# A two-layer graph network on one core: the output bias moves from VectorE to GpSimd, three opening loads change queue, and all steps get a new order

## The chip, the cores and the metric

The kernel runs on one core of a Trainium2 chip. The core has five engines with a queue of instructions each: TensorE (PE in the profile; its weight loads are listed as PEld), VectorE (DVE), ScalarE (ACT), GpSimd (POOL) and SyncE (SP), which here only issues DMAs. An engine works through its queue in order; engines wait for each other by semaphores. SBUF is the on-chip memory of 128 partitions, PSUM the banks that TensorE writes to. The metric is the device time of one execution in microseconds (us).

## The reference

The input is x, 128 graphs of 128 nodes with 256 features, and one 0/1 matrix adj of 128 x 128 for each graph. Everything is float32. Layer 0 is an attention block with 8 heads whose values depend on the adjacency, a residual and norm, and a Gelu feed-forward with 1024 hidden features. Layer 1 is two graph attention steps without a nonlinearity between them, a residual and norm, and a Relu feed-forward:

```python
def layer0(src, adj):
    q, k = heads(src @ Wq + bq), heads(src @ Wk + bk)
    attn = softmax(q @ k.T / sqrt(32))
    out = sum((attn * (adj == r)) @ heads(src @ Wv[r] + bv[r]) for r in range(4))
    x = ln(src + out @ Wo + bo, g1, beta1)
    return ln(x + gelu(x @ W1 + b1) @ W2 + b2, g2, beta2)

def gat(h, adj, W, a):
    Wh = h @ W
    e = leaky_relu(Wh @ a[:256] + (Wh @ a[256:]).T, 0.2)
    return softmax(where(adj > 0, e, NEG), axis=1) @ Wh

def layer1(x, adj):
    h = gat(gat(x, adj, W1, a1), adj, W2, a2)
    h = ln(x + h, g_ln1, b_ln1)
    return ln(h + relu(h @ w_ff1 + b_ff1) @ w_ff2 + b_ff2, g_ln2, b_ln2)
```

## The kernel before

The 16384 tokens are worked through in 32 groups of 4 graphs (512 tokens). A group passes through a fixed set of stages, each written as a Python generator that emits a few instructions per step:

- `in` loads the transposed x (xT, 512 KB), `rest` loads adj (256 KB) and then x (512 KB). All three are issued from SP's queue.
- `bo` is `prepared` (L687 on): two adds of the output bias to the incoming x, one for each pair of graphs, 128 x 512 elements each, in place, and a square of adj on ScalarE for a later check. The bias row `bo` has been enlarged by the value bias once at the start (`output_bias`). Its sum with x is the residual of the attention.
- `q` makes queries, keys and values. From group 2 on it is `projected`, with the seven-product scheme of Strassen and Winograd for a 2 x 2 split of each product (forms B11, B21, B22, T1 to T4 of a weight, L789).
- `a` is `attention`: scores into PSUM (ps, L859), exponentials on ScalarE (e, L866), the mask products `pm` = e times adj on VectorE (L876), the products with the values (pav, L975), reciprocals of the sums, the output product (pwo, L1021) and the add of the residual x (L416). `d` is `folded`, which sums the exponentials with copies by DMA.
- `n0` to `n3` are the norms: statistics (L407, L409), a root whose add is on VectorE (L430) and whose power is on GpSimd (L431), and two affine passes on VectorE (L445). `n0` to `n2` then copy x as two planes of 16 bits on ScalarE (L465) and transpose them by DMA from SP's queue (L468); `t0` to `t2` put the words together on ScalarE (yT, L493).
- `f` and `fc` are the two halves of the first feed-forward, `k` and `kc` of the second (products L525 and L534), again with the seven-product scheme. `seeded` is a PSUM bank that ScalarE fills with an earlier product before further products are added to it; `p` and `h` are copies and differences between the products.
- `l` is the graph attention layer (pw L1098, py L1111, pg L1124), `out` the store, `z` the last norm.

The order of the work is written out by hand as three strings of tokens, FRONT, STEADY and TAIL. A token such as `bo:1` asks for the next step of stage `bo` of the group that is one ahead of the current base; `*3` repeats. STEADY is run for bases 1 to 29. The strings fix the order of the instructions within each engine's queue; between engines only the data dependencies and the reuse of buffers hold. So several groups are in work at a time: in STEADY the second feed-forward of group g-1, the graph layer of group g, the first feed-forward of group g+1 and the projections and scores of group g+2 lie side by side.

At the start `Weights` issues the loads. Loads that are put in a list (`to("qk")` and so on) are issued one by one by tokens such as `Lqk` from SP's queue; bq, bk, the row of value biases, its first row as columns (b0) and bo are issued at once from ScalarE's queue before any token.

x has three buffers (pool `io`), adj three, xT one. GpSimd's queue holds, in a steady group, four powers and nothing else.

Of the kernel before, what the change touches and what calls it, by code (L numbers as in the profile page):

```python
# [120 lines left out]


FRONT = """
Lqk in:0 Lqk q:0 Lqk Lv q:0 L1 q:0 Lv q:0 Lqk L1 in:1 Lv q:0 Lv_ q:0*2 Lv q:0 rest:0 Lv_ a:0*3 L1
q:0 d:0 a:0 Lv_ a:0 d:0 a:0*2 d:0 L1*2 d:0 q:0 d:0*2 Lh1 d:0 a:0 d:0 a:0 q:0*2 rest:1 q:0*2
rest:0 wqk a:0*7 q:1 L2 w1 a:0 L4 a:0*3 q:1*2 d:0 bo:0 d:0 Lgat Lg1 a:0*2 d:0*2 q:1 L2 Lg1 d:0 w1
d:0 q:1 bo:0 q:1 q:0 d:0 Lo q:1 d:0 q:0 q:1 bo:0 a:0*4 L1 a:1 a:0*2 a:1 a:0 rest:1 wqk w1 a:0
a:1*2 a:0 a:1 L3 a:1 Lg1 d:1 a:0 d:1 Lg1 d:1 a:1 a:0*2 q:1 a:0*2 Lg2 d:1 Lgat n0:0 b1 d:1*2 L2
a:1 d:1 n0:0 q:1 b1 q:1 n0:0 L4 q:1 wqk d:1 q:1 Lgat n0:0 a:1 b1 output_bias n0:0 wv L2 q:1
n0:0*2 t0:0 b1 a:1 output_bias t0:0 a:1 Lh1*2 a:1*3 Lgat a:1*2 gw f:0 a:1 t0:0 a:1 b1 L3 a:1 b1  # L130
w2 a:1 t0:0 w1 t0:0*2 d:1 fc:0 b1 gw q:1 Lg2 d:1*3 a:1 f:0 fc:0 f:0 b1 f:0 a:1 fc:0*3 d:1 L4 d:1
f:0 q:1 fc:0 f:0 fc:0 f:0 d:1 f:0 Lh2 gw L3 a:1 f:0 d:1 a:1 f:0*2 a:1 fc:0 a:1 fc:0*2 bo:1 w2
bo:1 fc:0*2 a:1*3 f:0 a:1 wqk fc:0 in:2 fc:0 gw a:1 L3 f:0 a:1 fc:0 f:0 fc:0*2 a:1 f:0 w2 a:1 Lh1
bo:1 a:1 L3 a:1 f:0 fc:0*3 f:0 wv n0:1 L3 fc:0 q:2 f:0 fc:0 c1 fc:0 f:0 n0:1 q:2 fc:0 w2 n0:1
fc:0 q:2 n0:1 t0:1 n0:1 f:0 c1 t0:1 fc:0 f:0 L4 fc:0 c1 n0:1 fc:0 wv fc:0 f:0*2 n0:1 q:2 fc:0 q:2
f:0 fc:0*2 q:2 n1:0*2 gw n1:0 Lh2 n1:0 q:2 t0:1 n1:0*2 c1 n1:0 q:2 t0:1 c1 u1 f:1 q:2*3 t0:1 c1
f:1 t1:0*2 c1 l:0 gelu u2 fc:1 t1:0 l:0 t0:1 t1:0 l:0*2 fc:1 f:1 l:0 fc:1 l:0*2 fc:1 l:0 q:2 l:0
f:1*3 fc:1*3 f:1*3 fc:1 rest:2 fc:1*2 q:2*2 exp q:2 fc:1 l:0*2 u1 l:0 q:2 u1 q:2 f:1 q:2 l:0 fc:1
f:1 l:0 a:2 l:0 u2 l:0 fc:1 l:0*3 a:2 f:1 fc:1*2 a:2 l:0 fc:1 l:0 a:2*2 l:0*3 a:2 l:0*2 u2 u1 d:2
l:0 d:2 l:0 fc:1 f:1 l:0 f:1 wv f:1*2 fc:1*2 l:0 d:2 fc:1 l:0 d:2 f:1 a:2 l:0 u2 q:2 l:0 fc:1 c1  # L140
l:0*2 fc:1 q:2 l:0*2 f:1 l:0*2 d:2*2 l:0 q:2 fc:1 q:2*2 l:0 f:1 d:2 q:2 l:0*2 q:2 l:0*2 q:2 l:0
n2:0 q:2*2 d:2 n2:0 fc:1*2 q:2 f:1 n2:0*2 d:2 fc:1 n2:0*2 a:2 fc:1 f:1 n2:0 fc:1 q:2 t2:0 f:1
rest:2 t2:0 q:2 fc:1 t2:0*2 fc:1 k:0 a:2 q:2 a:2*3 d:2 fc:1 f:1 kc:0 a:2 d:2 t2:0 a:2 k:0 f:1 a:2
k:0 a:2 k:0 a:2 t2:0 fc:1 a:2 d:2*2 kc:0 a:2 kc:0 a:2 d:2 a:2 k:0 a:2 k:0 d:2 n1:1 a:2 d:2 a:2
k:0 n1:1 k:0 kc:0
# [4 lines left out]
k:-1*2 l:0*2 kc:-1 a:1*2 kc:-1 l:0 kc:-1 l:0 a:1 kc:-1 l:0 kc:-1*2 l:0*2 kc:-1 k:-1 a:1 n0:1  # L150
kc:-1 k:-1 n0:1*2 kc:-1 k:-1 n0:1 bo:1 n0:1 q:2 k:-1 kc:-1 n0:1*2 kc:-1 l:0 kc:-1 l:0 k:-1
kc:-1*2 q:2 l:0 q:2 l:0*2 t0:1*2 q:2 kc:-1 l:0 rest:2 f:1 k:-1 l:0 t0:1*2 q:2*2 l:0*2 fc:1 q:2
gelu l:0 t0:1 l:0 f:1*3 t0:1 l:0*2 fc:1 l:0 f:1 l:0*3 k:-1 q:2 f:1 fc:1 l:0 kc:-1 l:0 f:1 fc:1
f:1*2 q:2 n3:-1 l:0 fc:1*3 q:2 fc:1 f:1 fc:1*3 q:2 fc:1*2 f:1 q:2 f:1 q:2 n3:-1 fc:1*2 f:1*2 q:2
l:0 fc:1 l:0*2 f:1 q:2 l:0 fc:1*2 f:1 n3:-1 fc:1 l:0 q:2 fc:1 q:2*2 f:1 fc:1 out:-1 l:0 a:2 fc:1
l:0*2 f:1 l:0*2 a:2*2 l:0 a:2*2 l:0 d:2 q:2 a:2 q:2 d:2*2 f:1 a:2 fc:1 l:0*4 d:2 l:0 n2:0 q:2
d:2*2 q:2 fc:1*2 q:2 n2:0 q:2 f:1 n2:0*3 q:2 d:2 fc:1 q:2 n2:0 q:2 d:2 f:1 n2:0 fc:1*2 q:2 d:2
f:1 fc:1 q:2 t2:0*2 a:2 t2:0*2 q:2 a:2 q:2 f:1 q:2 fc:1 t2:0*2 k:0 f:1 exp a:2 fc:1 kc:0 d:2
a:2*2 rest:2 a:2 k:0 kc:0 d:2 a:2 k:0*2 kc:0 a:2 k:0 d:2*2 a:2 d:2 a:2 d:2 a:2 fc:1 a:2*4 d:2 a:2
# [3 lines left out]
n1:0 k:-1 kc:-1 n1:0*2 kc:-1 d:1*2 a:1 k:-1 kc:-1 a:1 d:1 k:-1 bo:1 a:1 kc:-1*4 d:1 kc:-1 n1:0
k:-1 n1:0 a:1 t1:0*2 k:-1 kc:-1 k:-1 l:0 bo:1 a:1 kc:-1 l:0*2 kc:-1 k:-1 l:0 kc:-1 a:1 t1:0 a:1
t1:0 l:0 a:1 k:-1 a:1 l:0 kc:-1*2 l:0*2 kc:-1 a:1 kc:-1 l:0 kc:-1 bo:1 k:-1 kc:-1*2 a:1*2 k:-1
kc:-1 n0:1*2 k:-1 n0:1*2 k:-1 n0:1 l:0 n0:1 l:0 n0:1 l:0 kc:-1 l:0 t0:1 k:-1 l:0 kc:-1 l:0 kc:-1
t0:1 kc:-1*2 l:0 k:-1 l:0 kc:-1 l:0 gelu l:0 f:1 t0:1 l:0 t0:1 k:-1 l:0 kc:-1 l:0 t0:1*2 l:0 f:1
fc:1*2 kc:-1 l:0 fc:1 f:1*2 k:-1 fc:1 f:1 n3:-1 l:0*2 fc:1 f:1*2 l:0 fc:1 n3:-1 l:0 fc:1 l:0 f:1
fc:1 f:1 l:0 fc:1 f:1 fc:1 l:0*2 fc:1 l:0 fc:1 l:0*3 fc:1*2 f:1*2 fc:1 f:1 l:0*4 fc:1 f:1 l:0
fc:1 f:1*2 fc:1 l:0*2 fc:1 l:0 fc:1 f:1 l:0*2 f:1 fc:1*2 n2:0 f:1 n2:0 fc:1*2 n2:0*2 fc:1 f:1  # L170
n2:0 f:1 n2:0*2 t2:0*2 fc:1*2 f:1 fc:1 t2:0 fc:1*2 f:1*2 fc:1*2 n1:1 t2:0 k:0 t2:0 k:0 kc:0 n1:1
t2:0 k:0 n1:1 k:0 n1:1 kc:0 n1:1 k:0 kc:0 n1:1*2 t1:1*2 kc:0 k:0*3 t1:1 k:0 l:1*2 t1:1 l:1 kc:0
n3:-1 l:1 kc:0*2 l:1*3 kc:0*2 l:1 kc:0 l:1 kc:0 k:0 kc:0 l:1*4 kc:0 l:1*3 k:0 l:1 kc:0 l:1 k:0*3
kc:0 l:1*5 kc:0 l:1 kc:0 k:0 l:1*5 k:0 l:1 kc:0 l:1 k:0 l:1*2 kc:0*3 l:1*2 kc:0 k:0 l:1*6 kc:0
k:0 l:1*3 kc:0 l:1*2 k:0 n2:1 kc:0 n2:1*5 kc:0*2 k:0 kc:0 n2:1 k:0 kc:0 k:0 t2:1*2 kc:0*2 k:1
t2:1*3 kc:1 t2:1 k:1 kc:1 k:1 checks k:1 kc:1 k:1 kc:1 k:1 kc:1 k:1 kc:1*2 k:1 kc:1*3 k:1 k:0
kc:1*2 kc:0 k:1*2 kc:1 k:1 kc:1*2 k:1 kc:1 k:1*2 kc:1 k:1*2 kc:1 n3:0 kc:1*2 k:1 kc:1 exp kc:1*2
n3:0*2 kc:1*2 out:-1 k:1*3 kc:1*3 k:1 kc:1 k:1 kc:1 out:0 k:1 z:1*2 kc:1*2 z:1*2
# [11 lines left out]
def fast_pass(ctx, tc, a, out):  # L190
# [494 lines left out]
    gelu, exp = lambda: table(AF.Gelu), lambda: table(AF.Exp)  # L685

    def prepared(S):  # L687
        g, xr, ad = S["g"], S["x"], S["ad"]
# [10 lines left out]
        yield 1
# [888 lines left out]
```

## Time and profile before

| | |
|---|---|
| time, median of 3 runs | 2611.95 us (2609.13 to 2613.82) |
| time of the profiled execution | 2611.15 us |
| its span | 2609.4 us |
| granted TensorE clock, mean | 0.997 |
| busy PE / PEld / DVE / ACT / POOL | 2566.4 / 2286.5 / 2329.3 / 1883.0 / 142.1 us |
| DMA, mean share and rate | 71 GB/s over 16 engines, 31% of their span |

The span is the time from the first to the last instruction of the profiled execution. Busy time is a union over an engine's instructions; matmuls are pipelined and their ends are modelled, so a matmul's listed duration is longer than the distance to the next one. A line of the timeline has the start, the duration, the engine, the line of the kernel, the operation, what it writes and reads, and the shape; in brackets stands the idle time of the engine before it and what ended it. A line of the groups has the number of instructions, then busy time and the mean ns of one, then the idle time before them.

### The profile page before, as it was taken

To read this page: it belongs to the slowest core of one execution; us is meant where nothing else is said; L and a number is where in the kernel's file an instruction comes from. 1 tells how busy PE (TensorE), PEld (TensorE's weight loads), DVE (VectorE), ACT (ScalarE), POOL (GpSimd) and SP (SyncE) were. 2 spreads that over 40 slices of the span, in tenths; PEclk is the share of its full clock that TensorE was granted. 3 is DMA by queue.
4 is the path that set the end of the run, shared out by engine and by line. 5 is a ranking of instruction groups with operands and counts; after the bars stand their busy time and mean duration, and the time that the engine had idled before them with its cause. 6 is when DMAs were issued, how large, how long until landed. Compare 5 with 4: busy or idle time off the path is not lost.

```text
span 2609.4 us, 54584 instructions
## 1 busy us (share of the span) xinstructions
PE 2566.4 (98%) x20362; PEld 2286.5 (88%) x20362; DVE 2329.3 (89%) x6041; ACT 1883.0 (72%) x3841; POOL 142.1 (5%) x137
## 2 busy tenths in 40 slices
...
DMA packets 317375, 186.36 MB, mean 71 GB/s; under 512 B 230448, under 2 KB 272560, under 8 KB 317104
## 3 DMA queue, kind: packets, MB, share of 16 engines
...
q8 instruction: 162, 2.65, 0.4%
...
## 4 chain that ended last, share of the span: by engine, by line
PE 83%; ACT 7%; DVE 5%; DMA 3%; issue 1%; SPq 1%; POOL 0%; DVEq 0%; ACTq 0%; POOLq 0%
PE ph L525 14%; PE po L534 14%; PE seeded L534 12%; PE seeded L525 11%; PE pqqa L789 4%; PE pvqa L789 4%; PE pav L975 4%; PE pw L1098 4%; PE pqqb L789 3%; PE pvqb L789 3%; PE pwo L1021 3%; ACT e L866 3%; PE ps L859 3%; PE pg L1124 2%; PE py L1111 2%; ACT hT L549 1%
## 5 line engine op out<-in xcount | busy, mean ns | idle before, releaser
L493 ACT COPY yT<-pT 128x512 uint16<-128x512 uint16 x384 | 271.3, 764 | 107.8 <-DMA pT<-planes 106.4
L465 ACT COPY planes<-x 128x512 uint16<-128x512 uint16 x384 | 218.3, 615 | 137.2 <-DVE x L445 135.5
L431 POOL TENSOR_TENSOR rs<-rs,mhalf 128x4 f32<-128x4 f32 x129 | 140.0, 1085 | 2406.7 <-DVE rs L430 1893.4
L525 PE MATMUL seeded<-yS,w_L_gnn_w_ff 128*128 128x256 f32 x768 | 203.5, 387 | 1.4 <-ACT p L629 0.7
L525 PE MATMUL seeded<-yS,w_L_gnn_W 128*128 128x256 f32 x768 | 199.9, 383 | 1.5 <-DVE hT L633 1.1
L525 PE MATMUL ph<-yT,w_L_gnn_W 128*128 128x256 f32 x768 | 198.1, 381 | 0.6 <-ACT yT L493 0.6
L407 DVE BATCH_NORM_STATS2 st<-x 128x6 f32<-128x256 f32 x512 | 190.1, 413 | 2.5
L534 PEld LDWEIGHTS po<-w_L_gnn_W,hT 128*128 128x128 f32 x1536 | 186.1, 192 | 6.7 <-ACT hT L549 2.1
L525 PE MATMUL ph<-yT,w_L_gnn_w_ff 128*128 128x256 f32 x768 | 187.7, 379 | 3.2 <-ACT seeded L648 2.1
L534 PE MATMUL po<-w_L_gnn_W,hT 128*128 128x128 f32 x1536 | 187.1, 275 | 1.7 <-ACT hT L549 1.7
L534 PE MATMUL po<-w_L_gnn_w_ff,hT 128*128 128x128 f32 x1536 | 187.1, 275 | 0.0
L534 PEld LDWEIGHTS po<-w_L_gnn_w_ff,hT 128*128 128x128 f32 x1536 | 181.7, 192 | 1.7
L525 PEld LDWEIGHTS seeded<-yS,w_L_gnn_w_ff 128*128 128x128 f32 x768 | 139.3, 190 | 38.2 <-ACT seeded L648 9.5
L876 DVE TENSOR_TENSOR pm<-e,adj 128x512 f32<-128x512 f32 x256 | 169.2, 682 | 0.4 <-ACT e L866 0.2
L525 PEld LDWEIGHTS seeded<-yS,w_L_gnn_W 128*128 128x128 f32 x768 | 142.8, 190 | 28.0 <-ACT seeded L648 6.4
L866 ACT ACTIVATE e<-ps 128x512 f32<-128x512 f32 x256 | 139.4, 602 | 34.8 <-PE ps L859 29.1
L525 PEld LDWEIGHTS ph<-yT,w_L_gnn_w_ff 128*128 128x128 f32 x768 | 143.5, 190 | 22.1 <-ACT seeded L648 2.5
L525 PEld LDWEIGHTS ph<-yT,w_L_gnn_W 128*128 128x128 f32 x768 | 141.7, 190 | 21.6 <-ACT seeded L621 1.2
L903 ACT COPY es<-e 32x512 f32<-32x512 f32 x240 | 147.1, 613 | 4.5
L549 ACT ACTIVATE hT<-hT,c_L_gnn_b_ff 128x256 f32<-128x256 f32 x256 | 115.9, 501 | 39.4 <-DVE hT L592 36.7
L621 ACT COPY seeded<-ph 128x512 f32<-128x512 f32 x64 | 37.4, 584 | 135.9 <-DVE x L667 135.2
L1098 PE MATMUL pw<-wu,yT 128*128 128x260 f32 x512 | 133.2, 389 | 2.3 <-ACT wh L1103 1.3
...
## 6 DMA issues: line engine op xcount, KB each, us to landing
...
es<-e SPq DMA_DIRECT2D x240, 64.0 KB, 2.0
pm<-e SPq DMA_DIRECT2D x240, 64.0 KB, 2.0
ea<-e SPq DMA_DIRECT2D x240, 64.0 KB, 2.0
...
```

The costliest lines, as they stand in the source:

```text
L407: nc.vector.bn_stats(st[:, b % 2, :], S["x"][:, b, :])
L431: nc.gpsimd.tensor_tensor(rs[:, bs], rs[:, bs], k.mhalf[:, bs], op=ALU.pow)
L465: nc.scalar.copy(planes[:, :, b], words)
L493: nc.scalar.copy(o.rearrange("p (b t h) -> p h b t", b=2, h=2), pT[:, :, :, c, :])
L525: nc.tensor.matmul(bank[:, s * TH : (s + 1) * TH], wa[:, form, 0, f * P : (f + 1) * P], m, start=start and s == 0, stop=True, skip_group_c ...
L534: nc.tensor.matmul(bank[:, s * P : (s + 1) * P], m[:, f, s * P : (s + 1) * P], wb_[:, form, f, :], start=start and s + f == 0, stop=True, ...
L549: nc.scalar.activation(o[:, s], o[:, s] if src is None else src[:, s * TH : (s + 1) * TH], func, bias=ba[:, f : f + 1],)
L789: nc.tensor.matmul(bank[:, s * TH : (s + 1) * TH], *ops, start=start and s == 0, stop=True, skip_group_check=True,)
L866: nc.scalar.activation(e[:, s], pss[s], AF.Exp, scale=SCALE)
L876: nc.vector.tensor_mul(pm[:, s], S["e", p][:, s], S["ad"][:, pair(p), None, :].to_broadcast([P, 2, NCH, P]),)
L903: nc.scalar.copy(es[own, 0], flat_e[own, s])
L1098: nc.tensor.matmul(pw[:, :NU], yT[:, c, b * P : (b + 1) * P], wu[:, c, :], start=(c == 0), stop=(c == NCH - 1),)
```

## The change

Three edits are made together.

1. In `prepared` the two adds of the bias are issued on GpSimd for groups 2 to 31, and on VectorE for groups 0 and 1 as before.
2. The load of xT of group 0 is split in two DMAs of 256 KB. The loads of the value biases' row, of b0 and of bo go from ScalarE's queue into a list of their own, `b`, whose three steps are issued from SP's queue by the token `Lb`.
3. FRONT, STEADY and TAIL are replaced. STEADY begins at another point of the group's cycle, with the end of `t2` and the values' last products, and holds the same steps.

```diff
@@ prepared
         for p in range(G // 2):
-            nc.vector.tensor_add(xr[:, pair(p)], xr[:, pair(p)], over(bo, 2))
+            (nc.vector if g < 2 else nc.gpsimd).tensor_add(
+                xr[:, pair(p)], xr[:, pair(p)], over(bo, 2)
+            )
@@ entered
-        nc.sync.dma_start(
-            xt, xT[:, g * T : (g + 1) * T].rearrange("(c p) t -> p c t", p=P)
-        )
+        cols = xT[:, g * T : (g + 1) * T].rearrange("(c p) t -> p c t", p=P)
+        for c in range(NCH) if g == 0 else (slice(0, NCH),):
+            nc.sync.dma_start(xt[:, c], cols[:, c])
@@ loads
     bq, bk = k.col("L0_gnn_bq"), k.col("L0_gnn_bk")
+    k.queue = nc.sync
+    to("b")
     bvs, bv = k.row("L0_gnn_bv", 2 * D, cut(2 * D)), k.tile([P, D], "bv")
     b0 = cut(NCH)
-    k.load(nc.scalar, b0, a["L0_gnn_bv"][0].rearrange("(c p) -> p c", p=P))
+    k.load(nc.sync, b0, a["L0_gnn_bv"][0].rearrange("(c p) -> p c", p=P))
     bo = k.row("L0_gnn_bo")
-    k.queue = nc.sync
     to("qk")
@@ FRONT (its first tokens)
-Lqk in:0 Lqk q:0 Lqk Lv q:0 L1 q:0 Lv q:0 Lqk L1 in:1 Lv q:0 Lv_ q:0*2 Lv q:0 rest:0 Lv_ a:0*3 L1
+in:0 Lqk Lv Lqk q:0 Lqk Lv q:0 Lqk q:0 in:1 Lv q:0*2 Lv_ q:0 L1 Lv q:0*2 rest:0 Lb a:0*2 Lb a:0
...
@@ STEADY before: the second attention's mask products, n1's root, the bias adds
-k:0 n1:1 kc:0 a:2 k:0 n1:1 k:0
-n1:0 k:-1 n1:0 kc:-1 n1:0 d:1*2 a:1 k:-1 kc:-1 d:1 a:1 kc:-1*2 bo:1 a:1 d:1 a:1 kc:-1 a:1*4
-kc:-1*3 n1:0 in:2 kc:-1 n1:0 k:-1 t1:0*2 kc:-1 k:-1*2 t1:0 k:-1 l:0*2 k:-1 kc:-1*2 bo:1 t1:0
...
@@ STEADY after: the same steps
+t2:-1 q:1 rest:1 t2:-1 fc:0 q:1 f:0 k:-1 a:1 q:1 d:1 a:1*2 fc:0 a:1 kc:-1 t2:-1 a:1 k:-1 d:1
+a:1*3 k:-1 t2:-1 kc:-1*2 d:1 a:1 d:1 k:-1*2 a:1 d:1 fc:0 k:-1 a:1*2 n1:0 a:1*2 k:-1 d:1*2 a:1*2
+n1:0 kc:-1 k:-1 n1:0*2 k:-1 kc:-1 k:-1 n1:0 d:1*2 a:1*2 kc:-1 d:1 a:1 kc:-1 bo:1 kc:-1 d:1 a:1
+kc:-1 a:1*3 rest:2 a:1 kc:-1*3 n1:0*2 k:-1 t1:0 kc:-1 k:-1 t1:0 kc:-1 k:-1*2 t1:0 l:0*2 t1:0 k:-1
+kc:-1 k:-1*2 l:0 kc:-1 in:2 l:0 bo:1 kc:-1 a:1*2 kc:-1 l:0 kc:-1 a:1 kc:-1 l:0*2 a:1 k:-1 l:0*2
...
```

More of the change, by code (lines that the diff above doesn't have):

```diff
@@ L123 @@
 FRONT = """
-Lqk in:0 Lqk q:0 Lqk Lv q:0 L1 q:0 Lv q:0 Lqk L1 in:1 Lv q:0 Lv_ q:0*2 Lv q:0 rest:0 Lv_ a:0*3 L1
[L125 to L145, printed above, removed]
+in:0 Lqk Lv Lqk q:0 Lqk Lv q:0 Lqk q:0 in:1 Lv q:0*2 Lv_ q:0 L1 Lv q:0*2 rest:0 Lb a:0*2 Lb a:0
+Lv_ a:0 L2 d:0 wqk a:0*2 d:0*3 q:0 L1 Lv_ q:0 a:0 L1 q:0*2 Lb d:0*2 a:0 q:0 rest:1 d:0*2 a:0 q:0
@@ new lines @@
+a:0*2 L1 a:0*4 L1 Lg1 a:0*3 q:1 a:0*2 q:1 Lgat d:0 rest:0 d:0 w1 a:0*2 q:1 q:0 Lgat L1 d:0*2 Lg2
+q:0 d:0 bo:0 q:1*2 d:0*2 Lo a:0 d:0 q:1*2 a:0*2 Lg1 a:0 L2 bo:0 q:1 a:1 wqk L4 w1 a:1 a:0 a:1*2
+Lg1 a:1 a:0*2 a:1 a:0 L2 a:0 Lg1 d:1*4 Lgat w1 a:1 a:0*2 Lh1 a:0*2 b1 a:0 d:1 q:1 n0:0 d:1 rest:1
+q:1 b1 q:1 n0:0 a:1 d:1 n0:0 q:1 n0:0 L4 d:1 L4 a:1 b1 n0:0*2 q:1 n0:0 b1 a:1 L2 q:1 L3 b1 t0:0*2
+a:1*2 gw w1 Lh1 f:0 a:1*2 Lh1 output_bias d:1 a:1*3 t0:0 d:1 output_bias Lg2 t0:0 a:1 t0:0 q:1
+d:1 b1 fc:0 f:0 t0:0 q:1 bo:0 fc:0 bo:1 fc:0 f:0 a:1 w2 a:1 f:0 b1 a:1 b1 f:0 fc:0 f:0 Lgat d:1
@@ new lines @@
+a:1 fc:0*2 w2 f:0 fc:0*2 f:0*2 d:1 Lh2 f:0 a:1 gw fc:0*4 f:0 d:1 L3 fc:0 d:1*2 f:0 a:1 fc:0 f:0
+w2 f:0 wv wqk fc:0 a:1*2 Lh1 L3 fc:0 f:0 fc:0 a:1*2 fc:0*2 a:1 f:0 a:1 bo:1 wv a:1 fc:0 a:1*3 f:0
+a:1 gw fc:0 in:2 q:2 rest:2 fc:0 q:2*2 a:1 n0:1 q:2 fc:0 f:0 fc:0 n0:1 L3*2 n0:1 L3 fc:0 n0:1 f:0
+n0:1 q:2 c1 w2 bo:1 q:2 n0:1 gw f:0*2 fc:0*4 f:0 n0:1 f:0 wv t0:1 f:0 fc:0 q:2 fc:0*2 t0:1*2 n1:0
+L4 t0:1 n1:0 gw Lh2 q:2 n1:0*2 c1 n1:0 f:1 n1:0*2 q:2 c1 u2 q:2 c1 t0:1 fc:1 q:2 c1 t1:0*2 t0:1
+c1 f:1 fc:1 u2 f:1 l:0*2 f:1 t1:0 l:0 t1:0 l:0*2 gelu fc:1 l:0*3 f:1 q:2 fc:1 l:0 f:1 fc:1*2 q:2
@@ L146 @@
+wqk fc:1 f:1 u1 f:1 fc:1 q:2 fc:1 q:2*2 exp u2 q:2*2 c1 l:0 fc:1 l:0 a:2 l:0*2 fc:1 l:0 a:2 f:1
+l:0 u1 f:1 a:2 q:2 l:0 d:2 fc:1 l:0 a:2 l:0*2 fc:1 a:2 l:0 u2 l:0*4 u1 wv l:0 fc:1 l:0*3 fc:1 l:0
+f:1 d:2 fc:1 d:2 c1 q:2 d:2 fc:1 a:2 u1 f:1*3 q:2 fc:1 f:1*2 fc:1 f:1 l:0*3 fc:1*2 q:2 a:2 l:0*2
+fc:1 l:0 q:2 f:1*2 fc:1 l:0 d:2*2 l:0 q:2 l:0*2 q:2 l:0 f:1 l:0 q:2 d:2 l:0 f:1 l:0*3 d:2 fc:1
+q:2 l:0 n2:0 fc:1*2 q:2 n2:0 d:2 n2:0 fc:1 n2:0 fc:1 n2:0*3 f:1 fc:1 t2:0 a:2 q:2 f:1 t2:0
 """
 STEADY = """
-n1:0 k:-1 n1:0 kc:-1 n1:0 d:1*2 a:1 k:-1 kc:-1 d:1 a:1 kc:-1*2 bo:1 a:1 d:1 a:1 kc:-1 a:1*4
@@ L149 @@
-kc:-1*3 n1:0 in:2 kc:-1 n1:0 k:-1 t1:0*2 kc:-1 k:-1*2 t1:0 k:-1 l:0*2 k:-1 kc:-1*2 bo:1 t1:0
[L150 to L159, printed above, removed]
-k:0 n1:1 kc:0 a:2 k:0 n1:1 k:0
+t2:-1 q:1 rest:1 t2:-1 fc:0 q:1 f:0 k:-1 a:1 q:1 d:1 a:1*2 fc:0 a:1 kc:-1 t2:-1 a:1 k:-1 d:1
```

42 lines of the change are left out of this document (26 added, 16 removed).

## The prediction

> **What bounds the kernel now.** I read the page's busy shares first, then three stretches of the span, then the chain that ended last, then one group's period in order of time.
>
> ```profile
> PE 2566.4 (98%) x20362; PEld 2286.5 (88%) x20362; DVE 2329.3 (89%) x6041; ACT 1883.0 (72%) x3841; POOL 142.1 (5%) x137
> ```
>
> ```profile
> 0.00:140.00 140.00, 127.64 (x997) 100.75 (x998) 97.63 (x263) 85.51 (x169) 6.18 (x11) 0.99 0.47 120
> 140.00:2440.00 2300.00, 2290.62 (x18309) 2054.93 (x18309) 2098.90 (x5418) 1700.65 (x3471) 125.70 (x116) 1.00 0.32 71
> 2440.00:2609.40 169.40, 148.12 (x1060) 130.83 (x1058) 132.77 (x362) 96.84 (x202) 10.23 (x10) 0.97 0.19 43
> ```
>
> The columns of the second fence are the stretch, its length, then busy time of PE, PEld, DVE, ACT, POOL, the granted clock, the DMA share and GB/s. PE is the bound: in the middle it is idle for 2300 - 2290.62 = 9.4 us. It is idle for 12.4 us in the opening and 21.3 us at the end. The matmuls are the same before and after, so the change can only move PE's idle time and its small delays.
>
> The chain shows the period, from one group's four exponentials to the next:
>
> ```profile
> 1645.28 2.05 ACT e L866 x4
> 1725.33 2.05 ACT e L866 x4
> 1804.47 2.05 ACT e L866 x4
> ...
> 2122.12 2.05 ACT e L866 x4
> 2201.11 2.06 ACT e L866 x4
> ```
>
> The shortest is 2201.11 - 2122.12 = 78.99 us; 1645 to 1725 takes 80.05. From 373.10 to 2438.65, 26 periods, the mean is 79.44. So at most some 0.45 us a group, 13 us over 29 steady groups, comes back if every group runs like the best one.
>
> The next view splits the group from 2045.1 us on into two stretches:
>
> ```profile
> 2045.10:2071.30 26.20, 26.01 (x240) 23.59 (x240) 25.72 (x66) 14.38 (x28) 1.42 (x2) 1.00 0.42 85
> 2071.30:2124.10 52.80, 52.77 (x393) 47.48 (x392) 46.70 (x125) 44.58 (x94) 2.91 (x3) 1.00 0.28 65
> ```
>
> For 26 us out of 79, DVE is as full as PE (25.72 of 26.20 us). This stretch runs from the second attention's product pg to the second pav (L975), and ends so:
>
> ```profile
> 2070.58 0.17 DVE L430 TENSOR_SCALAR rs<-mv 128x4 f32<-128x4 f32 x1
> 2070.65 0.69 DVE L876 TENSOR_TENSOR pm<-e,adj 128x512 f32<-128x512 f32 x1
> 2070.89 1.31 POOL L431 TENSOR_TENSOR rs<-rs,mhalf 128x4 f32<-128x4 f32 x1 [19.66 <-DVE rs L430]
> 2071.25 0.68 DVE L592 TENSOR_TENSOR hT<-ph,p 128x512 f32<-128x512 f32 x1
> 2071.39 0.16 PEld L975 LDWEIGHTS pav<-e,v 128*32 128x32 f32 x8 [0.33 <-issue]
> ```
>
> The last mask product pm ends at 2071.34, and PE begins pav at 2071.39. The first eighth of pav reads e alone, which gives some 0.25 us more. DVE work added ahead of pm there reaches PE.
>
> **The bias add (from group 2 on).** DVE loses two adds a group (L691: 64 instructions, median 0.682 us; in a full queue one starts 0.61 us after another). They stood after pav, at 2077.54 and 2085.04, in the second stretch, where DVE is idle for 6.1 of 52.8 us. PE waited for neither, so I credit nothing; at most the 1.2 us. POOL gains two adds of 128x512. The nearest rows:
>
> ```profile
> L431 POOL TENSOR_TENSOR rs<-rs,mhalf 128x4 f32<-128x4 f32 x127 | 138.2, 1088 | 2393.1 <-DVE rs L430 1879.8 <-DVE c_out L421 506.5 <-DVE c_L_gnn_b L349 6.8
> ...
> L87 POOL TENSOR_TENSOR r_L_gnn_beta<-r_L_gnn_beta,temp 128x256 f32<-128x256 f32 x1 | 0.7, 726 | 38.4 <-DMA temp<-in_L_gnn_b_dram 38.4
> ```
>
> An add of 256 takes 0.73 us, one of 512 between 0.73 and 1.45; I take 1.35 (twice 0.726, less one 0.10 of fixed cost, from POOL's 128x1 memsets). Two are 2.7 us on an engine that is 95% idle. What matters is when they run. The new list has the first `bo:1` after the third fold, but a list sets order within an engine only. On POOL the adds stand behind n1's power (L431) and wait only for x. Its load, `rest:1`, is issued some 10 us of PE work earlier and lands in 4.1 us (the page's row for x). So both adds run straight after n1's power, and n1's root stands just ahead of the second attention's mask products: rs, pm, pm, hT, pm, pm, then the affine of n1. That is the end of the full stretch.
>
> Does a POOL add hold up DVE there? The trace shows the reverse case. The power above took 1.31 us: it began while pm, with both inputs in SBUF, had 0.45 us to run. A power that begins beside an operation with one input in PSUM takes 1.01:
>
> ```profile
> 2090.36 0.42 DVE L606 TENSOR_TENSOR x<-po,x 128x256 f32<-128x256 f32 x1
> 2090.47 1.01 POOL L431 TENSOR_TENSOR rs<-rs,mhalf 128x4 f32<-128x4 f32 x1 [18.27 <-DVE rs L430]
> 2090.70 0.87 DVE L445 SCALAR_TENSOR_TENSOR x<-x,mv,r_L_gnn_g 128x256 f32<-128x256 f32 x2
> ```
>
> All 30 powers that began under a pm took 1.31 us; the 29 beside L606 and the 29 beside L819 took 1.01. So POOL waits for a DVE operation that reads two SBUF inputs. The trace has no long POOL read with such a DVE operation behind it (a power reads 4 elements a partition, and L445 beside it is not slowed), so DVE's loss has two ends.
> - Nothing, if POOL always gives way.
> - A whole block. Counted from rs: the power begins at 0.31, behind pm, and ends at 1.62. Add 1 runs from 1.62 to 2.97. The third pm, due at 1.9, waits 1.07 us and ends at 3.65. Add 2 then runs to 5.0, and the fourth pm waits 1.4 more: 2.47 us. At 83.53 us a power got its turn at the end of one such DVE operation though the next stood ready, so POOL can win there.
>
> The nearest row shows exclusion, so I take the first block whole (1.07). Whether the second falls on pm or on the affine behind it is open, so half of it (0.7). Cover: 0.25 us from pav's first part, and 0.25 because the new list has one matmul group more (T3, 0.86 us of PE) but also one DVE add more (0.61) ahead of pav. That is 1.77 - 0.5 = 1.27 us a group, between 0 and 2.0. Over 29 groups 37 us (0 to 58). Behind the waiting pm on DVE stand n1's affine, and behind that ACT's plane copies, the transposes and the graph layer's weights; they shift with it and PE waits once.
>
> The Trainium skill, "SBUF — State Buffer", section "Who interferes with whom", speaks against this change: GpSimd's SBUF ports are DVE's second pair, a GpSimd operation that reads SBUF contends with a DVE instruction that has two SBUF inputs, and whichever comes first holds the pair for its whole length while the other blocks fully. The 1.31 and 1.01 us rows agree for the one direction; for the other no row here does. By the rule alone both adds would block DVE whole, 2.0 us a group after the cover and some 58 us in all, where the rows alone allow anything from 0.
>
> **The order of the steps.** The tight places I compared: pg waits 0.21 us in 29 groups for the exponentials that free its bank; po, scores, po, pg keep their order, so the wait stays. n1's affine ends about 0.5 us later before the first B22 product of the second FFN, since T3 moved ahead of pav, and ACT's plane copies ahead of `act11` and the seed copy then press on T2 and T4 (there the copy p ended 0.34 us before T4 needed its bank). n0's root is issued ahead of h01 and h2 and is 1.4 us earlier against pwo, and f begins one product (0.86 us) later. The adj load (256 KB) goes from behind n0's transposes to ahead of n1's second; xT (512 KB) goes from ahead of that one to behind it; x's load leaves the queue ahead of the turned sums. The Gelu table load (1.28 us) moves behind p7, in the second stretch, where ACT is busy for 44.58 of 52.8 us. I can't sum these to a sign: between -0.45 us a group (every group like the best) and +0.5 (the plane copies), 0 taken, so -13 to +15 us. If ACT's cover were gone, the table load alone would be 1.28 us a group.
>
> **The opening.** PE works on its four warm-up products until 6.64 us and goes straight into q, so the halves of xT gain nothing. ACT waits from its last issue (2.77 + 0.49 us) until q's result at 8.39, so the three issues it loses gain nothing; SP gains four of some 0.45 us. v's bias now lands after adj's load, near 15 us by 10.5 for its issue and 4.7 to landing; DVE first reads it at 15.31; bo, behind it, is first read at 27.93. Cost 0, between -2 and 3 us.
>
> **Sum.** The profiled execution took 2611.15 us (span 2609.4 and 1.75 around it), 0.8 below the median. 2611.15 + 37 + 0 + 0 = 2648; against the median, 2649.
>
> **Rivals.**
> - The blocking is small or hidden, and the order pays. Then DVE has 1.2 us less, groups run like the best, -13 us, and up to -5 from opening and end: about 2595. For it: POOL is idle 95%, and L445 ran beside a power at full speed. Against: DVE's full stretch held no bias add, so nothing is taken out of it. It decides if a POOL add costs DVE less than the 0.5 us cover.
> - No blocking, but the new order's plane copies delay T2 and T4 by 0.5 us a group: +15, about 2627. For it, the 0.34 us of slack at T4.
> - The adds on POOL are simply hidden and the order is worth nothing: within 0.2%, 2612. (0.2%, 5 us, is what a measurement of this kernel can tell.)
>
> **How the numbers follow.** Forecast 0.55 (own range 2633 to 2670: half of 2.47 us less the cover, 0.74 a group, and the whole, 2.0), order's stalls 0.15, faster 0.24, hidden 0.06. Slower is 0.55 + 0.15 = 0.70. The range takes in half of the faster case, down to 2596, and the whole block with some of the order's stalls, up to 2680.
>
> **What would show it.** Right: DVE's pm (L876) above 0.68 us, or gaps ahead of it, while POOL's L691 runs; L691 on POOL straight behind L431, 1.2 to 1.5 us long; PE idle ahead of pav on pm; a period near 80.7. Wrong: pm at 0.68 beside the add and a period of 79.4 or less; or L691 on POOL late, beside DVE work with PSUM inputs.

## The result, and the profile after

| | before | after |
|---|---|---|
| time, median | 2612.2 us (2609.1 to 2613.8, 4 runs) | 2650.6 us (2650.0 to 2654.8, 4 runs) |
| profiled execution, its span | 2611.15, 2609.4 us | 2650.76, 2649.0 us |

The ratio is 1.015, with a 95% interval of 1.0137 to 1.0163: 38.4 us slower. In the code of after, the lines behind `prepared` are two higher (pm L876 is L878, pav L975 is L977); up to L691 they are the same.

The busy shares of after, from its page:

```profile
PE 2575.1 (97%) x20362; PEld 2296.4 (87%) x20362; DVE 2353.9 (89%) x5981; ACT 1875.7 (71%) x3841; POOL 237.8 (9%) x197
```

DVE issues 60 instructions fewer and yet is busy for 24.6 us longer (2329.3 before). That is the first sign: moving work away has made the rest of DVE's work longer. The same three stretches as before (stretch, length, busy time of PE, PEld, DVE, ACT, POOL, granted clock, DMA share, GB/s):

```profile
0.00:140.00 140.00, 130.71 (x1018) 104.04 (x1018) 98.49 (x264) 85.16 (x169) 5.47 (x11) 0.99 0.47 120
140.00:2440.00 2300.00, 2257.67 (x18026) 2026.47 (x18025) 2090.48 (x5268) 1662.66 (x3404) 217.12 (x172) 1.00 0.31 70
2440.00:2649.00 209.00, 186.74 (x1322) 165.89 (x1320) 164.92 (x452) 127.86 (x269) 15.19 (x14) 0.97 0.20 43
```

PE is now idle for 2300 - 2257.67 = 42.3 us of the middle, where it was 9.4. The clock is unchanged. The loss is spread evenly over the groups; the chain shows the period:

```profile
214.86 2.05 ACT e L868 x4
295.59 2.05 ACT e L868 x4
```

It is 80.73 us, and most groups have this very value: measured from one group's first product pg to the next one's, 22 of the 28 full periods take 80.72 to 80.74 us (mean 80.79; before: shortest 78.98, mean 79.42). The groups and the waits name the place. First three of the pages' groups, pm before and then pm and pav after (busy, mean ns of one, idle time before them and who ended it), then the first rows of PE's list of waits (total us, times, longest):

```profile
L876 DVE TENSOR_TENSOR pm<-e,adj 128x512 f32<-128x512 f32 x256 | 169.2, 682 | 0.4 <-ACT e L866 0.2
L878 DVE TENSOR_TENSOR pm<-e,adj 128x512 f32<-128x512 f32 x256 | 220.7, 890 | 3.8 <-ACT e L868 3.5
L977 PE MATMUL pav<-pm,v 128*32 128x128 f32 x2048 | 125.1, 273 | 22.1 <-DVE pm L878 21.9
```

```profile
PE pav L977 <- DVE pm L878: 21.9, 30, 1.0
PE seeded L525 <- DVE hT L633: 15.4, 31, 1.5
```

A mask product pm takes 890 ns in the mean where it took 682, and PE waits for it 30 times, once for each group that has the adds on GpSimd. The second wait, on hT, is new too: hT L633 stands behind pm and n1's affine in DVE's queue. One group in order of time:

```profile
1128.43 0.16 DVE L430 TENSOR_SCALAR rs<-mv 128x4 f32<-128x4 f32 x1
1128.50 1.28 DVE L878 TENSOR_TENSOR pm<-e,adj 128x512 f32<-128x512 f32 x2
...
1128.73 1.31 POOL L431 TENSOR_TENSOR rs<-rs,mhalf 128x4 f32<-128x4 f32 x1 [17.75 <-DVE rs L430]
...
1129.80 0.69 DVE L592 TENSOR_TENSOR hT<-ph,p 128x512 f32<-128x512 f32 x1
1130.02 2.95 POOL L691 TENSOR_TENSOR x<-x,r_L_gnn_bo 128x512 f32<-128x512 f32 x2
...
1130.41 3.11 DVE L878 TENSOR_TENSOR pm<-e,adj 128x512 f32<-128x512 f32 x2
...
1133.57 0.30 PE L977 MATMUL pav<-pm,v 128*32 128x128 f32 x1 [0.72 <-DVE pm L878]
...
1135.03 0.68 DVE L633 TENSOR_TENSOR hT<-seeded,p 128x512 f32<-128x512 f32 x1
...
1135.76 1.13 PE L525 MATMUL seeded<-yS,w_L_gnn_w_ff 128*128 128x256 f32 x4 [0.47 <-DVE hT L633]
```

GpSimd goes straight from n1's power into the two adds, at 1130.02. The first two mask products, ahead of them, take 1.28 us together; the third and fourth, beside them, 3.11. Narrower windows give each alone: the adds start at 1130.02 and 1131.24 and take 1.27 and 1.73 us; pm starts at 1130.41 and 1131.76 and takes 1.43 and 1.76. So the third pm ends 0.55 us after the first add, and the fourth 0.55 us after the second (1131.29 and 1131.84; 1132.97 and 1133.52). The second add, on its side, is 0.46 us longer than the first: it stood beside the third pm. The two engines take turns: add, pm, add, pm.

### The profile page after: what moved, and what is told of

It is laid out like the page before. It is cut to its first block, busy times and chain, and to the rows that moved or that the text cites. A ratio compares the mean times of both kernels' runs of the same rounds, so it can differ in the third digit from the quotient of the medians.

```text
span 2649.0 us, 54711 instructions
## 1 busy us (share of the span) xinstructions
PE 2575.1 (97%) x20362; PEld 2296.4 (87%) x20362; DVE 2353.9 (89%) x5981; ACT 1875.7 (71%) x3841; POOL 237.8 (9%) x197
## 4 chain that ended last, share of the span: by engine, by line
PE 75%; DVE 18%; ACT 4%; issue 1%; DMA 1%; SPq 0%; POOL 0%; DVEq 0%; ACTq 0%; POOLq 0%
PE po L534 14%; PE seeded L534 11%; PE seeded L525 11%; PE ph L525 10%; DVE pm L878 5%; PE pw L1100 4%; PE pwo L1023 4%; PE pqqa L791 4%; PE pvqa L791 3%; PE pqqb L791 3%; ACT e L868 2%; PE pvqb L791 2%; DVE x L445 2%; PE pg L1126 2%; PE py L1113 2%; PE ps L861 1%
## 5 line engine op out<-in xcount | busy, mean ns | idle before, releaser
L431 POOL TENSOR_TENSOR rs<-rs,mhalf 128x4 f32<-128x4 f32 x129 | 147.9, 1146 | 2349.0 <-DVE rs L430 1822.5
L878 DVE TENSOR_TENSOR pm<-e,adj 128x512 f32<-128x512 f32 x256 | 220.7, 890 | 3.8 <-ACT e L868 3.5
L525 PE MATMUL seeded<-yS,w_L_gnn_w_ff 128*128 128x256 f32 x768 | 204.0, 388 | 18.2 <-DVE hT L633 15.0
L525 PE MATMUL seeded<-yS,w_L_gnn_W 128*128 128x256 f32 x768 | 200.0, 383 | 1.9 <-ACT seeded L648 1.1
L525 PE MATMUL ph<-yT,w_L_gnn_W 128*128 128x256 f32 x768 | 197.1, 379 | 0.0
L525 PE MATMUL ph<-yT,w_L_gnn_w_ff 128*128 128x256 f32 x768 | 192.3, 384 | 0.0
L525 PEld LDWEIGHTS seeded<-yS,w_L_gnn_w_ff 128*128 128x128 f32 x768 | 140.6, 190 | 52.2 <-DVE hT L633 23.6
L525 PEld LDWEIGHTS seeded<-yS,w_L_gnn_W 128*128 128x128 f32 x768 | 142.8, 190 | 28.9 <-ACT seeded L648 8.3
L525 PEld LDWEIGHTS ph<-yT,w_L_gnn_w_ff 128*128 128x128 f32 x768 | 143.9, 191 | 26.5 <-ACT p L584 8.0
L525 PEld LDWEIGHTS ph<-yT,w_L_gnn_W 128*128 128x128 f32 x768 | 145.4, 190 | 19.8
L868 ACT ACTIVATE e<-ps 128x512 f32<-128x512 f32 x256 | 132.5, 602 | 33.3 <-PE ps L861 30.6
L977 PE MATMUL pav<-pm,v 128*32 128x128 f32 x2048 | 125.1, 273 | 22.1 <-DVE pm L878 21.9
```

The source lines that it names most:

```text
L431: nc.gpsimd.tensor_tensor(rs[:, bs], rs[:, bs], k.mhalf[:, bs], op=ALU.pow)
L525: nc.tensor.matmul(bank[:, s * TH : (s + 1) * TH], wa[:, form, 0, f * P : (f + 1) * P], m, start=start and s == 0, stop=True, skip_group_c ...
L868: nc.scalar.activation(e[:, s], pss[s], AF.Exp, scale=SCALE)
L878: nc.vector.tensor_mul(pm[:, s], S["e", p][:, s], S["ad"][:, pair(p), None, :].to_broadcast([P, 2, NCH, P]),)
L977: nc.tensor.matmul(pav[s * DH : (s + 1) * DH, u, c, :], v[:, d0 : d0 + DH], m[:, s, u, c, :], start=(r == 0), stop=(r == 1),)
```

## The experiments

My theory after this: GpSimd's two adds cost time only because of what DVE does beside them, and they make the whole loss. The rivals: the new order or opening makes part of it; an add on GpSimd costs DVE the same wherever it stands; what counts is that PE or another engine waits for the adds' result.

**All adds back on VectorE.** The new order and the new opening stay.

```diff
-            (nc.vector if g < 2 else nc.gpsimd).tensor_add(
+            nc.vector.tensor_add(
```

> The changed kernel with all bias adds back on VectorE; the opening loads and the new order stay. My theory (the two GpSimd adds hold the mask products pm): pm (L876) back to 0.68 us, no wait of pav for pm, none of the first B22 product for hT, so the period falls from 80.73 by the two waits of some 0.9 and 0.8 us to about 79.0, and the time to 2595 to 2605 us. Rival (the order itself, with one more VectorE add ahead of pm, costs the time): the waits at pav stay, 2635 us or more.

Measured: 2613.2 us (2611.3 to 2615.0), ratio to before 1.0005, interval 0.9996 to 1.0015.

```profile
L876 DVE TENSOR_TENSOR pm<-e,adj 128x512 f32<-128x512 f32 x256 | 166.9, 681 | 5.0 <-ACT e L866 4.7
```

pm is at 681 ns, and no wait on pm is left. All of the loss, 2650.6 - 2613.2 = 37.4 us or 30 times 1.25, comes from the adds on GpSimd. The order and the opening together are worth nothing; the gain of 7 to 17 us that this expectation gave them isn't there.

**The opening alone.** The kernel before, with its order, and of the change only the second edit, the loads of the opening; the three `Lb` are put at the like places of the old FRONT (the third `Lb`, and the split of xT, stand in what is left out here).

```diff
-Lqk in:0 Lqk q:0 Lqk Lv q:0 L1 q:0 Lv q:0 Lqk L1 in:1 Lv q:0 Lv_ q:0*2 Lv q:0 rest:0 Lv_ a:0*3 L1
+Lqk in:0 Lqk q:0 Lqk Lv q:0 L1 q:0 Lv q:0 Lqk L1 in:1 Lv q:0 Lv_ q:0*2 Lv q:0 rest:0 Lb Lv_ a:0*2 Lb a:0 L1
...
+    k.queue = nc.sync
+    to("b")
...
-    k.load(nc.scalar, b0, a["L0_gnn_bv"][0].rearrange("(c p) -> p c", p=P))
+    k.load(nc.sync, b0, a["L0_gnn_bv"][0].rearrange("(c p) -> p c", p=P))
...
```

> The kernel before with the new opening alone: gnn_bv's two loads and gnn_bo's on SyncE's queue behind the first x, xT of group 0 loaded in two pieces, the old order otherwise. My prediction put the opening at -2 to +3 us and took 0. Theory: the first pg comes within 0.5 us of before and the time within 3 us, 2609 to 2615 us. Rival (the opening gains 3 us, PE's idle time there being 9.3 us instead of 12.4, and the new order loses them again, since the two together were worth nothing): 2606 to 2609 us.

Measured: 2614.5 us (2612.3 to 2617.5), ratio 1.0013, interval 1.0004 to 1.0022. The first pg came at 141.1 us where it was 137.9, so that part of the expectation missed. These are single profiles, though, and the first pg also moves between profiles with one and the same opening: 137.9 to 139.1 us with the old one, 138.0 to 140.8 with that of the change. The rival's gain of 3 us is excluded: in the old order the new loads cost some 2 to 3 us (the interval reaches from 1 to 6). Against the 1.0005 of the run before, no effect of the new order can be told apart from nothing.

**GpSimd only writes.** Adds on VectorE; in their place GpSimd fills a 128x128 tile with zeros, six times a pair (groups 2 to 27). The tile is made anew afterwards.

```diff
+            if 2 <= g < NG - 4:
+                for _ in range(6):
+                    nc.gpsimd.memset(k.ident, 0.0)
+            elif g == NG - 4 and p == 0:
+                make_identity(nc, k.ident)
```

> As the kernel with the bias on VectorE, but where GpSimd's adds stood GpSimd writes zeros to a 128x128 table 6 times per pair of graphs, for groups 2 to 27 (the identity table, which nothing reads in that time; it is made anew behind). Some 2.4 us a group of GpSimd work that reads nothing from SBUF, in the same place of its queue. Theory (GpSimd's reads of SBUF are what holds VectorE): within 3 us of the kernel with the bias on VectorE, pm at 0.68 us. Rival (any GpSimd operation beside VectorE holds it, or GpSimd's own queue does): 2630 us or more, pm longer than 1 us.

Measured: 2612.6 us, ratio 1.0007 (0.9997 to 1.0017).

```profile
1117.58 3.08 POOL L694 MEMSET ident<- 128x128 f32 x12
1117.98 1.28 DVE L881 TENSOR_TENSOR pm<-e,adj 128x512 f32<-128x512 f32 x2
1119.17 0.88 DVE L445 SCALAR_TENSOR_TENSOR x<-x,mv,r_L_gnn_g 128x256 f32<-128x256 f32 x2
```

GpSimd is busy for 3.08 us at the same place, about as long as with the two adds, and pm and the affine keep their durations. A busy GpSimd isn't enough; writing to SBUF isn't either.

**GpSimd reads, and nobody waits for it.** Adds on VectorE; GpSimd multiplies a 128x128 tile by itself, three times a pair.

```diff
+            if 2 <= g < NG - 4:
+                for _ in range(3):
+                    nc.gpsimd.tensor_mul(k.ident, k.ident, k.ident)
```

> As the kernel with the bias on VectorE, but where GpSimd's adds stood GpSimd multiplies the 128x128 identity table by itself (0 and 1 keep their values) 3 times per pair of graphs, groups 2 to 27: some 2.5 us a group with two reads from SBUF, whose result nobody waits for. Theory: pm is held as in the changed kernel, 25 or 26 groups of 1.2 to 1.7 us: 2630 to 2650 us. Rival (the cost comes from the bias add's data, waits or place in x, not from the reads): within 5 us of the kernel with the bias on VectorE.

Measured: 2620.4 us (2618.1 to 2621.2), ratio 1.0035 (1.0022 to 1.0048).

```profile
1118.94 3.75 POOL L694 TENSOR_TENSOR ident<-ident 128x128 f32<-128x128 f32 x6
1119.32 1.49 DVE L879 TENSOR_TENSOR pm<-e,adj 128x512 f32<-128x512 f32 x2
1120.73 1.16 DVE L445 SCALAR_TENSOR_TENSOR x<-x,mv,r_L_gnn_g 128x256 f32<-128x256 f32 x2
1121.81 1.16 DVE L445 SCALAR_TENSOR_TENSOR x<-x,rs,r_L_gnn_beta 128x256 f32<-128x256 f32 x2
```

Nothing waits for these products, and still pm is 1.49 us for two instead of 1.28 and the affine 1.16 instead of 0.88: 0.21 + 2 x 0.28 = 0.77 us of DVE a group. So GpSimd's products, which read SBUF, hold DVE where its zeros, which only write, did not, and who waits for the result plays no part. The size missed the expected 2630 us: the six products hold DVE for 0.77 us where the two adds hold it for 1.83, since the first product fell beside L592, which reads PSUM, and the others are short.

**The adds in the old order.** The kernel before, with nothing but the adds of groups 2 to 31 on GpSimd.

```diff
-            nc.vector.tensor_add(xr[:, pair(p)], xr[:, pair(p)], over(bo, 2))
+            (nc.vector if g < 2 else nc.gpsimd).tensor_add(
+                xr[:, pair(p)], xr[:, pair(p)], over(bo, 2)
+            )
```

> The kernel before, its order and its opening, with the bias adds from group 2 on moved to GpSimd and nothing else. There the adds of a group stand behind n1's power too, and x is loaded a little later in the group. Theory (the adds alone make the loss, in either order): 2640 to 2675 us, with some DVE instruction of two SBUF inputs near 1.4 to 1.8 us and TensorE waiting behind it. Rival (the loss needs the new order, which puts the adds beside the mask products): within 8 us of the kernel before, 2604 to 2620 us.

Measured: 2669.0 us (2666.9 to 2669.9), ratio 1.0218 (1.0201 to 1.0235).

```profile
1138.25 1.31 POOL L431 TENSOR_TENSOR rs<-rs,mhalf 128x4 f32<-128x4 f32 x1 [19.66 <-DVE rs L430]
1138.62 0.68 DVE L592 TENSOR_TENSOR hT<-ph,p 128x512 f32<-128x512 f32 x1
1139.22 1.90 DVE L445 SCALAR_TENSOR_TENSOR x<-x,mv,r_L_gnn_g 128x256 f32<-128x256 f32 x2
1139.54 2.70 POOL L691 TENSOR_TENSOR x<-x,r_L_gnn_bo 128x512 f32<-128x512 f32 x2
1141.04 1.88 DVE L445 SCALAR_TENSOR_TENSOR x<-x,rs,r_L_gnn_beta 128x256 f32<-128x256 f32 x2
...
1143.57 1.13 PE L525 MATMUL seeded<-yS,w_L_gnn_w_ff 128*128 128x256 f32 x4 [1.79 <-DVE hT L633]
```

Here pm is through when the adds begin (682 ns in the mean), and n1's affine is hit: each pair of passes takes 1.9 us where it takes 0.87, and PE waits 1.79 us for hT behind it. The same two adds cost 57.8 us in the old order and 37.4 in the new one. The period says less of this difference than the time does: 17 of 29 periods take 80.91 to 80.93 us, only 0.2 us more than with the change. Some 10 us go with the clock. In this profile the granted clock falls to half for 3.4 us six times between 150 and 2450 us, and the six periods in which this happens take 82.53 to 83.09 us; in the kernel before and with the change it does so not once in that stretch. The other executions agree: the mean granted clock is 0.993 or 0.994 in all four, and 0.997 or 0.998 with the change. Why the clock falls here no run shows. What is shown is which instruction is held: the one of two SBUF inputs that stands beside the adds.

**The first add alone on GpSimd**, the second pair's on VectorE, in the new order.

```diff
-            (nc.vector if g < 2 else nc.gpsimd).tensor_add(
+            (nc.vector if g < 2 or p else nc.gpsimd).tensor_add(
```

> The changed kernel with the add of the first pair on GpSimd and that of the second pair on DVE. The singly read mask products say what each add holds: 0.75 us for the first (1.43 against 0.68), 1.08 us for the second (1.76 against 0.68), 1.83 together, of which 1.25 us a group reach the time. Theory: the third pm is near 1.43 us, the fourth at 0.68 us; of the 0.75 us some 0.25 us are covered by pav's first part, so 0.4 to 0.6 us a group, 2624 to 2633 us. Rival (the end of the second add alone sets the time, the first is covered): 2613 to 2618 us. Rival (the adds' queue does not matter, each costs half): 2632 us.

Measured: 2619.1 us (2617.5 to 2621.2), ratio 1.0027 (1.0015 to 1.004).

```profile
1117.40 1.27 POOL L691 TENSOR_TENSOR x<-x,r_L_gnn_bo 128x512 f32<-128x512 f32 x1
1117.79 2.03 DVE L878 TENSOR_TENSOR pm<-e,adj 128x512 f32<-128x512 f32 x2
...
1122.06 1.13 PE L525 MATMUL seeded<-yS,w_L_gnn_w_ff 128*128 128x256 f32 x4 [0.47 <-DVE hT L633]
```

The hold is as expected: 2.03 - 1.28 = 0.75 us. The time is not: 5.9 us above the run with both adds on VectorE, 0.2 us a group. The periods show why. With both on VectorE the shortest period is 79.07 us, but they are irregular, with a mean of 79.59: PE loses another half microsecond a group at changing places behind pav (pw L1098, and the seeded products L525 after it). With the first add on GpSimd 17 of 28 periods are 79.64 or 79.65 (mean 79.71). The stall, PE's wait for hT, is there in each group and adds 0.57 us to the shortest period; most of the irregular part is gone. So the first add isn't covered, as the first rival has it, although the time lies just above that rival's range. I read this as work that was late for PE now and then (planes, loads) being in time when PE comes later; the periods show the sum, and no run was made for the cause of it.

**The adds later, by a later load.** The new order with x's load, and only that, moved later in STEADY, so that the adds wait for x.

```diff
-t2:-1 q:1 rest:1 t2:-1 fc:0 q:1 f:0 k:-1 a:1 q:1 d:1 a:1*2 fc:0 a:1 kc:-1 t2:-1 a:1 k:-1 d:1
-a:1*3 k:-1 t2:-1 kc:-1*2 d:1 a:1 d:1 k:-1*2 a:1 d:1 fc:0 k:-1 a:1*2 n1:0 a:1*2 k:-1 d:1*2 a:1*2
+t2:-1 q:1 t2:-1 fc:0 q:1 f:0 k:-1 a:1 q:1 d:1 a:1*2 fc:0 a:1 kc:-1 t2:-1 a:1 k:-1 d:1
+a:1*3 k:-1 t2:-1 kc:-1*2 d:1 a:1 d:1 k:-1*2 a:1 d:1 rest:1 fc:0 k:-1 a:1*2 n1:0 a:1*2 k:-1 d:1*2 a:1*2
```

> The changed kernel, but the load of the next group's x (512 KB) is issued behind the last copies of the turned sums instead of ahead of them, so that the GpSimd adds, which wait for nothing else, run some 18 to 22 us into the period, beside transposes, reductions and reciprocals, and not beside pm. Theory: pm at 0.68 us, pav waits no longer, the time near that of the kernel with the bias on VectorE, 2595 to 2612 us, a few us more if folds or h differences are held instead. Rival (a GpSimd add costs VectorE the same wherever it runs, or the late load is missed by the residual add): 2635 us or more.

Measured: 2663.9 us (2661.7 to 2666.2), ratio 1.0203 (1.0186 to 1.022). pm is back at 687 ns and the wait on it gone, and still the time is worse: a new wait took its place, of PE on yT. Either the late load makes it, or the adds at their new place. **The late load with all adds on VectorE** tells these apart:

```diff
-t2:-1 q:1 rest:1 t2:-1 fc:0 q:1 f:0 k:-1 a:1 q:1 d:1 a:1*2 fc:0 a:1 kc:-1 t2:-1 a:1 k:-1 d:1
+t2:-1 q:1 t2:-1 fc:0 q:1 f:0 k:-1 a:1 q:1 d:1 a:1*2 fc:0 a:1 kc:-1 t2:-1 a:1 k:-1 d:1
...
-            (nc.vector if g < 2 else nc.gpsimd).tensor_add(
+            nc.vector.tensor_add(
```

> All bias adds on DVE, as in e1_dve, and x's load as late as in e4_x_late: GpSimd has no add at all from group 0 on. Theory (the late load by itself costs e4_x_late its time, as its 512 KB go ahead of the turned planes on the DMA engines): the wait of pw on yT (2.6 us at most, some 1.5 us a group) is there again, 2645 to 2670 us. Rival (GpSimd's adds beside the later DVE work cost it): no such wait, near 2613 us as e1_dve.

Measured: 2665.9 us (2664.3 to 2668.1), ratio 1.0211 (1.0194 to 1.0228). First PE's wait and SP's queue with the load moved and the adds on VectorE, then SP's queue with the adds on VectorE and the load where the change put it:

```profile
PE pw L1098 <- ACT yT L493: 44.7, 29, 2.8
```

```profile
573.03 0.59 SPq L225 DMA_DIRECT2D x<-in_x_dram  x1
573.72 1.25 SPq L468 DMA_TRANSPOSE pT<-planes  x1
...
578.61 1.38 ACT L493 COPY yT<-pT 128x512 uint16<-128x512 uint16 x2 [2.05 <-DMA pT<-planes]
...
579.42 1.33 PE L1098 MATMUL pw<-wu,yT 128*128 128x260 f32 x4 [1.49 <-ACT yT L493]
```

```profile
1120.84 2.26 SPq L468 DMA_TRANSPOSE pT<-planes  x1
...
1124.97 1.38 ACT L493 COPY yT<-pT 128x512 uint16<-128x512 uint16 x2 [0.40 <-DMA pT<-planes]
```

The load makes it. Its 512 KB are issued just ahead of n1's transpose; from the transpose's issue to ACT's first copy it takes 4.89 us instead of 4.13 (4.84 instead of 3.67 in the mean of 28 groups), the issue itself stands behind the load's 0.59 us, and PE waits 1.49 us. In four more periods the granted clock falls to half for 3.4 us, and they take some 2 us more than the others (82.98 to 83.94). That explains the miss: the edit undid one stall and made another.

**The adds later, with x loaded early.** The new order, with a copy of one column ahead of the first add in GpSimd's queue; the column is written by DVE when the second pair's sums are ready. `bo:1` moves one step of `d` later.

```diff
+    late = k.tile([P, 1], "late")
...
+            if p == 0 and 2 <= g < NG - 1:
+                nc.gpsimd.tensor_copy(late, c_att[:, 1, g, 1:2])
             (nc.vector if g < 2 else nc.gpsimd).tensor_add(
...
-n1:0 kc:-1 k:-1 n1:0*2 k:-1 kc:-1 k:-1 n1:0 d:1*2 a:1*2 kc:-1 d:1 a:1 kc:-1 bo:1 kc:-1 d:1 a:1
+n1:0 kc:-1 k:-1 n1:0*2 k:-1 kc:-1 k:-1 n1:0 d:1*2 a:1*2 kc:-1 d:1 a:1 kc:-1 kc:-1 d:1 bo:1 a:1
```

> The changed kernel, but GpSimd's two adds of a group start some 8 us later: a copy of one column (128x1) of c_att stands ahead of the first add in GpSimd's queue, and c_att is written by DVE (L918, L919) once the second pair's sums are turned; the first bo:1 stands one step of d:1 later in the list. x is loaded as early as in the changed kernel. The adds then run beside the reciprocal, the stream transposes, oT and the affines of pwo, which read one SBUF input, a few elements, or PSUM. Theory (the adds cost time only by where they stand: beside the mask products): pm back at 0.68 us on average, no wait of pav on pm, period near 79.5 us, 2605 to 2620 us. Rival (an add on GpSimd costs DVE the same anywhere in the group, and DVE has no slack for it): a new wait of TensorE on DVE, 2635 us or more.

Measured: 2608.0 us (2606.3 to 2609.6), ratio 0.9988 (0.9979 to 0.9998).

```profile
1121.94 0.18 POOL L693 COPY late<-c_att 128x1 f32<-128x1 f32 x1 [10.23 <-DVE c_att L924]
1122.08 2.97 POOL L694 TENSOR_TENSOR x<-x,r_L_gnn_bo 128x512 f32<-128x512 f32 x2
1122.13 0.71 DVE L1005 STREAM_TRANSPOSE rd<-rc 128x512 f32<-128x512 f32 x1
1122.76 1.15 DVE L642 TENSOR_TENSOR h<-hT 128x512 f32<-128x512 f32 x1
1123.83 0.74 DVE L1013 TENSOR_TENSOR oT<-pav,rd 128x256 f32<-128x256 f32 x2
1124.50 0.67 DVE L417 TENSOR_TENSOR x<-pwo,x 128x512 f32<-128x512 f32 x1
```

The same two adds, 2.97 us long, now cost no time. The transpose with one input and the two forms with an input in PSUM (pav, pwo) keep the durations that they have with the adds on VectorE (0.71, 0.75, 0.68); only h, whose inputs are both in SBUF, is held (1.15 us, 0.65 otherwise), once in each of 29 groups, and PE has no wait behind it. pm is at 684 ns, the shortest period 79.07, the mean 79.36. This version is 42.6 us faster than the change and 3 us faster than the kernel before; the interval just excludes no change.

**The same in the old order.** The kernel before, with the adds on GpSimd held back in the same way.

```diff
-n1:0 k:-1 n1:0 kc:-1 n1:0 d:1*2 a:1 k:-1 kc:-1 d:1 a:1 kc:-1*2 bo:1 a:1 d:1 a:1 kc:-1 a:1*4
+n1:0 k:-1 n1:0 kc:-1 n1:0 d:1*2 a:1 k:-1 kc:-1 d:1 a:1 kc:-1*2 a:1 d:1 bo:1 a:1 kc:-1 a:1*4
```

> The kernel before, its order and opening, with the adds of groups 2 to 30 on GpSimd and held back as in e6_pool_late: behind a copy of one column of c_att, and the first bo:1 one step of d:1 later. e2_pool_old, the same without holding back, took 2669 us. Theory (only the place on the clock matters): no affine of n1 at 1.5 us, h<-hT near 1.14 us beside the first add instead, period back near 79.3 us, 2604 to 2612 us: at or a little below the kernel before. Rival (moving the adds to GpSimd costs in the old order whatever they stand beside): 2630 us or more.

Measured: 2610.3 us (2607.6 to 2611.6), ratio 0.9992 (0.9983 to 1.0002). As expected, h is held instead (1.14 us in the median, once in 29 groups), and n1's affine is back at 0.48 us. Holding the adds back by some microseconds gives back 58.7 us, the old order's whole loss, and the granted clock is back at 0.996 to 0.998. Two orders, one cause: the place beside DVE's work with two SBUF inputs ahead of something that PE waits for.

## Why the prediction was right

The forecast was 2649 us, 37 above before; it came to 2650.6, 38.4 above. Step by step:

- *Where the adds run.* Right: L691 stands straight behind L431 on GpSimd, beside the third and fourth mask products, and PE waits ahead of pav. The signs that I named (pm above 0.68, PE idle on pm, a period near 80.7) are all there; the period is 80.73.
- *The add's length*, 1.35 us taken: 1.27 measured, and 1.73 for the second, which waits for pm in its turn.
- *The first block*, 1.07 us taken: 0.75 measured. The add began 0.03 us earlier after rs and was 0.08 shorter, pm was due 0.08 later, and 0.13 us of pm's 0.68 passes beside the add (the held pm ends 0.55 us after it).
- *The second block*, 1.4 us of which I took half, since I left open whether it falls on pm or on the affine: 1.08 measured, and wholly on pm. In the old order the affine took both blocks.
- *The cover*, 0.5 us taken: 1.83 us of DVE became 80.73 - 79.07 = 1.66 us of period, so 0.17. Neither pav's first part nor the T3 product gave what I counted.
- *What came back.* I had no term for it: the irregular half microsecond a group, 79.59 - 79.07 = 0.52, shrinks to 80.79 - 80.73 = 0.06. So the net is 1.66 - 0.46 = 1.20 us a group, against the 1.27 of my sum. Blocks 0.06 too small, cover 0.33 too large, this term missing: the sum is nearer than its parts, because two errors offset each other. That the forecast came within 2 us is in part luck.
- *One wait.* I wrote that the work behind pm shifts with it and PE waits once. PE waits twice a group, at pav for pm (0.72 us in the group shown) and again for hT L633 (0.47). With the first add alone on GpSimd only the wait for hT is left, so the one that I named needs the second block too.
- *DVE's two removed adds*, credited with nothing, at most 1.2 us a group. The held-back version against all adds on VectorE, 79.36 to 79.59 in the mean, shows a gain of some 0.2 us a group, what the held h costs taken off; in the old order it is 0.1 (79.32 to 79.41).
- *Order and opening*, 0 taken: right for the two together (ratio 1.0005). But the order isn't an independent term. With the adds on GpSimd, the new one is 18.4 us better than the old (2650.6 and 2669.0). Some 10 us of this go with the half-clock stretches of the old order's run. The rest, some 0.2 us a group, goes with the place: beside pm in the new order, beside the affine in the old one.
- *The rivals.* The faster one asked that an add cost DVE less than its cover: 1.83 us against 0.17 excludes it. The one with T2 and T4 delayed by the order alone is excluded by the run with all adds on VectorE.

The Trainium skill, "SBUF — State Buffer", section "Who interferes with whom", says that a DVE instruction with two SBUF inputs contends with a GpSimd instruction that reads SBUF, not with one that only writes, and that DVE instructions with at most one SBUF input, outside the 2-port performance modes, don't contend. The runs agree on each point: adds and products hold pm (1.43 and 1.76, 0.89 us), zeros don't (1.28 us for two), and the forms with PSUM inputs aren't held. The full block for a whole instruction, which the page has in its section "SBUF: two separate sides", fits but for 0.13 us: pm, 0.68 us long by itself, ends 0.55 us after the add and not with it.
